# A two-layer graph kernel: the second pass in a written order, one more column chunk by lists, and the own-row logits in layer two

## The chip, the cores and the metric

The kernel runs on one core of one Trainium2 chip. Its time is the device time of one execution in microseconds (us), the median of several runs. Before the change it is 734.61 us, the median of three runs.

## The reference, cut to what matters

The graph has 3327 nodes, padded to 3328 = 26 blocks of 128; `adj` is sparse with denser first rows and columns. A node has 512 features.

```
h  = relu(layernorm(x))
x1 = x + adj @ (relu(adj @ (h @ W1) + b1) @ W2) + b2       # layer one, 128 hidden features
h1 = relu(layernorm(x1))
attn_a = sigmoid([adj @ h1, h1] @ Wa + ba);  attn_b likewise with Wb, bb
e  = where(adj != 0, exp(-leaky_relu(s_left[i] + s_right[j])), 0)   # s = (h1 @ W_sa) @ a_sa
x_a = e / (rowsum(e) + 1e-5) @ (h1 @ W_sa);  x_b = adj @ (h1 @ W_gcnb) + b_gcnb
out = x1 + sigmoid(attn_a * x_a + attn_b * x_b)
```

## The kernel before

The transposed matrix `adjT` lies in DRAM. Everything is float32, except the small tables from which lists are made. Columns are taken in chunks of 512, with one chunk of 256; `back` is their order, from the right to the left. Tile pools and dependencies are set by a scheduler: `queued(x)` puts what is written under it behind instruction x in its engine's order, `high_priority` ahead of others, and `pace(g, m)` makes a DMA wait for a matmul.

*First pass.* Rows of x are normalised and multiplied by W1 while chunk 0 is worked on. Then for each chunk the 26 blocks of `adjT` are loaded (`load_adj`, SyncE's queue, 256 KB each) and multiplied (`acc_u`, L568) into g = relu(adj @ u + b1), which `make_g` keeps and also stores to DRAM. VectorE takes for each block the largest value in every 32 columns (`most`, L572). From `most` of a finished chunk `make_lists` builds, during the next chunk, lists of the rows that have something in a group of 32 columns: VectorE flags and counts (L443 to L459), TensorE and VectorE turn the counts into row numbers (`at` L502, `p_list` L513, `past` to `row_a`, L519 to L532). GpSimd then gathers those pieces of `adjT` by indirect DMA (`ae`, L166). `rooms[i]` is the number of lists of 64 rows that a block has; a block in `OWN` (`extra` 1) takes its own diagonal block whole instead. If a list overflows, a fallback at the end computes everything again.

*Second pass.* `listed_chunks` are the first `LISTED` = 2 chunks of `back`: for them adj @ g is summed from the gathered pieces and gathered rows of g (`list_sums`, `acc_s`, L784). The others, `dense_chunks`, are loaded again and multiplied (`acc_g`, L825): five chunks, 130 products. For each finished chunk a generator `make_h1` makes its rows of layer two: load x and add b2 (L650), multiply by W2 (`px`, L663), add (L666), normalise (`ln_relu`: bn_stats, Sqrt, Relu), take two scores with `w_rows` (L623), store x1 and the row h (`store_row`), own logits with `w_own` (L630) for the blocks outside `OWN` and `LATE`, and turn the scores (`pl`, L687). Between the dense products the loop calls `next_late`, `next(summing)`, `next(hubs)` and `make_e_hub` by fixed counts. `add_hubs` sums block 0 of layer two (the hub, dense in every row) from `a_hub` and `e_hub` (`acc_hub`, L709). ScalarE goes back and forth between Sqrt for rows and Exp for `e_hub`.

*Layer two.* The other blocks go from 25 down to 1. For block i `attend` gathers the rows of h by list (`hr` or `rows`, 266 KB each pair half), makes e with `s_left` and stores it beside the adjacency in `ae`; `sums` multiplies (`acc`, L981); `turn` transposes (`ptt`, L995) and VectorE copies (`tyT`, L1010); `weigh` multiplies by `W_g_sb` (`p_b`, L1035) and `W_sa_sb` (`p_a`, L1042); `finish` makes the output. TensorE's order is: weigh one block, turn the next, sum a third. `fetch_ae` gathers two more pieces of `ae` a block.

Of the kernel before, what the change touches and what calls it, by code (L numbers as in the profile page):

```python
# [9 lines left out]
F32 = mybir.dt.float32  # L10
# [15 lines left out]
EH = 8  # L26
SEG = 4
WAKE = 14
LISTED = 2
LN_EPS = 1e-5  # L30
SUM_EPS = 1e-5
# [7 lines left out]
LATE = 10, 11, 16  # L39

OWN = 1, 6, 7, 8, 12, 13, 14, 15, 17, 18


def list_rooms(n_blocks):

    rooms = [0, 8, 7, 6, 5, 5] + 6 * [4]
    return (rooms + n_blocks * [3])[:n_blocks]
# [3 lines left out]
def kernel(  # L51
# [24 lines left out]
    if NP % CW:  # L76
        back.append((0, NP % CW))
    listed_chunks = back[:LISTED]
    ND = listed_chunks[-1][0]
    dense_chunks = [(c0, min(CW, ND - c0)) for c0 in range(0, ND, CW)]  # L80
    made_order = []
    for k, c in enumerate(dense_chunks):
        for c0, w in (c, *listed_chunks[k : k + 1]):
            made_order += range(c0 // P, (c0 + w) // P)
# [3 lines left out]
    extra = [int(i in OWN) for i in range(NB)]  # L88
# [29 lines left out]
    bab_row = kept([P, 2], "bab_row")  # L118
    w_own = kept([P, 2, D], "w_own")
# [20 lines left out]
    def segments(i):  # L140

        r = rooms[i] + extra[i]
        n = -(-r // SEG)
        cuts = [-(-r * k // n) for k in range(n + 1)]
        return list(zip(cuts, cuts[1:]))
# [50 lines left out]
    def load_own(i):  # L196

        n = segments(i)[0][1]
        for h in range(2):
            rows = slice(i * P + h * HALF, i * P + (h + 1) * HALF)  # L200
            nc.scalar.dma_start(
                ae[i][h * HALF : (h + 1) * HALF, 0 : n + 1 : n, :GW],
                adjT[rows, rows].rearrange("j (q i) -> j q i", i=GW),
            )
# [41 lines left out]

    def masked_exp(e, adj):
# [11 lines left out]
    with (  # L259
        tc.tile_pool(name="l0", bufs=1) as l0,  # L260
        tc.tile_pool(name="l0w", bufs=2) as l0w,
        tc.tile_pool(name="adjp", bufs=8) as adjp,
    ):

        def load_adj(j, c, name, n=1):

            c0, w = c
            t = adjp.tile([P, CW], F32, tag="adj", name=f"{name}_{c0}_{j}")
# [19 lines left out]
        def load_hub(k):  # L288
            rows = slice(k * NB // HUB_LOADS * P, (k + 1) * NB // HUB_LOADS * P)
            nc.scalar.dma_start(  # L290
# [4 lines left out]
        def load_weights():  # L295
            nc.scalar.dma_start(W2_sb, W2)
            nc.scalar.dma_start(b2_row, b2.partition_broadcast(P))
            nc.scalar.dma_start(W_sa_sb, W_sa.rearrange("(k p) f -> p k f", p=P))
            nc.scalar.dma_start(w_own, w_self.partition_broadcast(P))
            nc.scalar.dma_start(bab_row, b_ab.partition_broadcast(P))  # L300
# [6 lines left out]
        def load_x(i):  # L307
            xs[i] = l0w.tile([P, D], F32, tag="x", name=f"x_{i}", bufs=5)
            x_loaded[i] = nc.sync.dma_start(xs[i], x[i * P : (i + 1) * P, :])
# [46 lines left out]
        def kept0(shape, name, dtype):  # L356
            return l0.tile(shape, dtype, tag=name, name=name)
# [16 lines left out]
        def make_constants():  # L374
# [36 lines left out]
            for r in sorted(set(rooms[1:])):  # L411
                i0, n = rooms.index(r), rooms.count(r)
# [9 lines left out]
                )  # L422
            yield
# [9 lines left out]
        def make_lists(nth, most):  # L433
# [5 lines left out]
            def small(shape, name, dtype, bufs=2):  # L439
                return l0w.tile(shape, dtype, tag=name, name=f"{name}_{c0}", bufs=bufs)  # L440

            flag = small([P, MG, NB], "flag", BF16)
            nc.vector.tensor_scalar(flag[:, :n, :], most[:, :n, :], 0.0, None, op0=ALU.is_gt)  # L443
            for b in range(w // P):
                if extra[c0 // P + b]:
                    groups = slice(b * NQ, (b + 1) * NQ)
                    own = flag[:, groups, c0 // P + b]
                    nc.vector.tensor_tensor(own, own, apart, ALU.mult)

            upto = small([P, MG, NB], "upto", BF16)  # L450
            flat = "p b j -> p (b j)"
            nc.vector.tensor_tensor_scan(
                upto[:, :n, :].rearrange(flat), begin[:, :n, :].rearrange(flat),
                flag[:, :n, :].rearrange(flat), 0.0, op0=ALU.mult, op1=ALU.add,
            )
            count = small([P, MG], "count", BF16)
            nc.vector.tensor_copy(count[:, :n], upto[:, :n, NB - 1])
            after = small([P, MG, NB], "after", BF16)
            nc.vector.tensor_tensor(  # L459
                after[:, :n, :], count[:, :n].unsqueeze(2).to_broadcast([P, n, NB]),  # L460
                upto[:, :n, :], ALU.subtract,
            )
# [5 lines left out]
            nc.vector.tensor_copy(offset[:, :n], p_off[:, :n])  # L468
# [10 lines left out]
            nc.vector.tensor_tensor(  # L479
                step[:, :n, :NB], p_sh[:, : n * NB].rearrange("p (b j) -> p b j", j=NB),  # L480
                upto[:, :n, :], ALU.add,
            )
# [7 lines left out]
            for batch in batches:  # L490
# [6 lines left out]
                at = l0w.tile([P, CW // NT, 2, HALF], BF16, tag="at", name=f"at_{f0}")  # L497
# [20 lines left out]
                past = l0w.tile([P, CW // NT, NB], BF16, tag="past", name=f"past_{f0}", bufs=1)  # L518
# [4 lines left out]
                jb = l0w.tile([P, CW // NT], F32, tag="jb", name=f"jb_{f0}")  # L523
# [25 lines left out]
        for n, c in enumerate(back):  # L549
            c0, w = c  # L550
            acc = bank(psA, f"acc_u_{c0}")
            per = CW // w
            most = l0w.tile([P, MG, NB], F32, tag="most", name=f"most_{c0}")
            for j in range(NB):
# [9 lines left out]
                if j % per == 0:  # L564
                    with queued(x_loaded[min(j + 4, NB - 1)] if n == 0 else None):
                        tile_a = load_adj(j, c, "a1", per)
# [755 lines left out]
```

## Time and profile before

| what | us |
|---|---|
| median of three runs (731.07 to 735.44) | 734.61 |
| profiled execution | 834.5 |
| its span | 832.8 |
| first pass, chunk 0 (0 to 62) | 62 |
| first pass, the rest (62 to 237) | 175 |
| second pass and hub's end (237 to 490) | 253 |
| layer two (490 to 833) | 343 |
| TensorE busy | 735.6 |
| VectorE busy | 506.0 |
| GpSimd busy | 461.1 |

The profile is one execution, and it took 100 us more than the median of the runs. In the names of its lines L568 is line 568 of the kernel before. A float32 product on TensorE shows as two records. The recorded length of a matmul is modelled, so the distance between starts says more than the length.

### The profile page before, as it was taken

What the parts mean: (1) busy time and instruction counts of PE and PEld (TensorE: products, weight loads), DVE (VectorE), ACT (ScalarE), POOL (GpSimd) and SP (SyncE); (2) the same over time, 40 slices, a digit from 0 to 9 for tenths busy, and PEclk for the clock granted to TensorE, in tenths of its full rate; (3) what the DMA queues carried; (4) which work ended last, traced back from release to release, by engine and by line L of the source; (5) the groups of instructions that cost most, each with busy time, mean ns of one, the idle gap of its engine ahead of it and who ended that gap; (6) DMA issues with size and microseconds to landing.
All of it is one profiled execution on the core that took longest, in us unless ns stands there. A gap on an engine that the chain in (4) does not pass through costs nothing.

```text
span 832.8 us, 11907 instructions
## 1 busy us (share of the span) xinstructions
PE 735.6 (88%) x3595; PEld 404.5 (49%) x3595; DVE 506.0 (61%) x1625; ACT 194.5 (23%) x402; POOL 461.1 (55%) x490
## 2 busy tenths in 40 slices
PE   9999888989899771999899749967999999999995
PEld 7774333444543220444355236633656655665554
DVE  7778868898860611798987225523665557553552
ACT  7770000000000110354544002211212222221121
POOL 2201756766657776534456766674657666767500
PEclk9999989999999875999999969996999999999999
DMA  8788988988878844789994755664667877767510
GB/s 271 245 287 259 326 246 242 293 272 246 232 232 284 262 132 134 240 279 312 327 314 135 241 150 145 199 185 115 195 211 244 255 206 233 240 205 234 178 51 29
DMA packets 104889, 185.08 MB, mean 222 GB/s; under 512 B 18401, under 2 KB 35441, under 8 KB 104818
## 3 DMA queue, kind: packets, MB, share of 16 engines
q1 hardware_dynamic: 66544, 113.43, 41.8%
q0 software_dynamic: 23264, 57.64, 24.3%
q10 hardware_dynamic: 15010, 13.18, 4.9%
q8 instruction: 30, 0.49, 0.2%
q14 instruction: 41, 0.34, 0.1%
HBM read 162.29 MB, written 22.26 MB: 222 GB/s over the span
## 4 chain that ended last, share of the span: by engine, by line
PE 72%; DVE 7%; issue 6%; another core or an unknown queue 6%; DMA 5%; ACT 2%; POOL 1%; SPq 1%; DVEq 0%; ACTq 0%; POOLq 0%
PE acc_u L568 17%; PE acc L981 12%; PE p_b L1035 11%; PE p_a L1042 10%; PE acc_g L825 8%; PE pu L333 3%; PE ptt L995 3%; DMA a<-in_adjT_dram 2%; PE acc_hub L709 2%; PE px L663 2%; PE pt L325 1%; DMA xb<-in_x_dram 1%; PE acc_s L784 1%; DMA hr<-h_rows,row_h 1%
## 5 line engine op out<-in xcount | busy, mean ns | idle before, releaser
L166 POOL DMA_INDIRECT ae<-in_adjT_dram,row_a x194 | 202.6, 1044 | 181.8 <-DVE past L519 54.3
L568 PE MATMUL acc_u<-a,rows 128*128 128x512 f32 (+1 forms) x364 | 161.0, 583 | 0.5 <-DMA a<-in_adjT_dram 0.5
L166 POOL DMA_INDIRECT hr<-h_rows,row_h x120 | 122.7, 1022 | 62.5 <-issue 27.4
L825 PE MATMUL acc_g<-a,g 128*128 128x512 f32 (+1 forms) x260 | 117.1, 584 | 7.2 <-DMA a<-in_adjT_dram 6.8
L572 DVE TENSOR_REDUCE most<-a 128x16 f32<-128x512 f32 (+1 forms) x182 | 112.3, 638 | 11.6 <-issue 6.3
L1035 PE MATMUL p_b<-W_g_sb,tyT 128*128 128x257 f32 x416 | 99.3, 391 | 15.8 <-DVE tyT L1010 15.3
L1035 PEld LDWEIGHTS p_b<-W_g_sb,tyT 128*128 128x128 f32 x416 | 77.8, 192 | 46.5 <-DVE tyT L1010 15.6
L166 POOL DMA_INDIRECT rows<-h_rows,row_h x74 | 75.1, 1015 | 44.3 <-PE acc L981 20.9
L568 PEld LDWEIGHTS acc_u<-a,rows 128*128 128x128 f32 x364 | 67.2, 195 | 58.8 <-issue 56.0
L1042 PE MATMUL p_a<-W_sa_sb,tyT 128*128 128x512 f32 (+2 forms) x216 | 94.2, 577 | 0.2
L1010 DVE COPY tyT<-ptt 128x512 f32<-128x512 f32 x51 | 34.8, 685 | 87.0 <-PE p_a L1042 31.7
L825 PEld LDWEIGHTS acc_g<-a,g 128*128 128x128 f32 x260 | 50.0, 200 | 58.5 <-issue 44.9
L981 PE MATMUL acc<-hr,ae 64*64 64x512 f32 x480 | 68.3, 614 | 4.4 <-issue 4.0
L166 POOL DMA_INDIRECT g_row<-g_rows,row_h x48 | 49.0, 1021 | 20.9 <-issue 13.4
L1042 PEld LDWEIGHTS p_a<-W_sa_sb,tyT 128*128 128x128 f32 x216 | 40.7, 189 | 38.8 <-issue 36.9
L884 ACT ACTIVATE f<-f 128x2 f32<-128x2 f32 x26 | 5.3, 203 | 192.4 <-DVE f L883 97.2
L981 PEld LDWEIGHTS acc<-hr,ae 64*64 64x64 f32 x480 | 27.6, 136 | 33.6 <-issue 33.0
L343 ACT ACTIVATE gT<-acc_u,b_col 128x512 f32<-128x512 f32 (+1 forms) x7 | 4.6, 656 | 163.8 <-DMA a<-in_adjT_dram 90.9
L663 PE MATMUL px<-W_sb,sT 128*128 128x512 f32 x52 | 26.7, 650 | 15.4 <-ACT sT L799 12.0
L666 DVE TENSOR_TENSOR xb<-px,xb 128x512 f32<-128x512 f32 x26 | 17.3, 682 | 36.6 <-PE px L663 28.5
L981 PE MATMUL acc<-rows,ae 64*64 64x512 f32 x296 | 37.1, 593 | 2.5 <-issue 2.3
L623 DVE SCALAR_TENSOR_TENSOR junk<-rows,w_rows 128x512 bf16<-128x512 f32 x52 | 35.6, 684 | 3.2 <-ACT rows L244 1.1
(159 smaller groups left out, 945.2 us busy)
## 6 DMA issues: line engine op xcount, KB each, us to landing
a<-in_adjT_dram SPq DMA_DIRECT2D x286, 256.0 KB
h_rows<-rows SPq DMA_DIRECT2D x26, 260.0 KB
x<-in_x_dram SPq DMA_DIRECT2D x26, 256.0 KB
xb<-in_x_dram SPq DMA_DIRECT2D x26, 256.0 KB
x<-xb ACTq DMA_DIRECT2D x26, 256.0 KB
x1b<-x SPq DMA_DIRECT2D x26, 256.0 KB
out_dram<-va SPq DMA_DIRECT2D x25, 256.0 KB
ae<-in_adjT_dram,row_a POOLq DMA_INDIRECT x194
```

Of the source, the lines that this page charges most:

```text
L166: return nc.gpsimd.indirect_dma_start(out=dst, out_offset=None, in_=table, in_offset=bass.IndirectOffsetOnAxis(ap=rows, axis=0), bounds_ch ...
L333: nc.tensor.matmul(pu[:, :HID], hT[:, k, :], W1_sb[:, k, :], start=(k == 0), stop=(k == KD - 1))
L568: added = nc.tensor.matmul(acc[:, :w], u[j], a[:, :w], start=(j == 0), stop=(j == NB - 1))
L572: nc.vector.tensor_reduce(most[:, : w // GW, j], a[:, :w].rearrange("p (b i) -> p b i", i=GW), axis=AX.X, op=ALU.max, apply_absolute_value ...
L623: return nc.vector.scalar_tensor_tensor(junk, h, 1.0, w_rows[:, s, :], op0=ALU.mult, op1=ALU.mult, accum_out=into)
L663: last_row[2] = nc.tensor.matmul(px, sT[:, b * P : (b + 1) * P], W2_sb, start=True, stop=True)
L825: added = nc.tensor.matmul(acc[:, :w], g[j], a[:, n % per, :], start=(n == 0), stop=(n == NB - 1))
L981: added = nc.tensor.matmul(taken[i]["acc"][h][q * HALF : (q + 1) * HALF, :], both[half_p, q * n + k, :], taken[i][k0][k][half_p, q, :D], s ...
L995: moved = nc.tensor.transpose(pt[:, k * P : (k + 1) * P], ty[h][:, k * P : (k + 1) * P], ident)
L1010: last = nc.vector.tensor_copy(dst, src)
L1035: nc.tensor.matmul(p_b[n][:, :WH], tyT[:, k, 0, :], W_g_sb[:, k, n * WH : (n + 1) * WH], start=(k == 0), stop=(k == KD - 1),)
L1042: last = nc.tensor.matmul(p_a[:, c0:c1], tyT[:, k, 1, :], W_sa_sb[:, k, c0:c1], start=(k == 0), stop=(k == KD - 1),)
```

## The change

- `LISTED` goes from 2 to 3: columns 1792 to 2303 are summed from lists. Four dense chunks and three listed ones are left, 104 dense products. Blocks 9, 21 and 24 (`TOP`) take besides their own block also the upper half of block 0 whole (`g_top`, `h_top`, `extra` 2), and their rooms shrink to 3, 2 and 2. The last 256-column part and its neighbour change places: the chunks at 256 and 768 are swapped in `back`.
- First pass: `load_adj` takes 512 KB; `most` is taken for two blocks in one instruction; the flags and counts of `make_lists` get high priority on VectorE, and lists start from row 4 (`LISTS_FROM`) of the next chunk instead of row 2. The loads of W2, W_sa (in four), the hub's column (in five) and the own blocks are issued one by one behind matmuls over the pass (`load_behind`), not together at a chunk's end.
- Second pass: the order of dense products `d`, list sums `s`, `t`, rows `x`, turned scores `l`, hub products `h` and `e_hub` `e` is written out in `PLAN`, and TensorE keeps it. A gather is issued for each 1.4 us of planned TensorE time. x is loaded ahead into eight buffers. A row's sum comes with the addition, its squares from ScalarE, and Ln and Exp replace Sqrt, in one table set. Only five blocks take their left score here, and none its own logits.
- Layer two: hub products, the turn and p_b of block 0 are interleaved before the sums of blocks 25 and 24, and p_a of block 0 follows those. Each block loads its own row (`load_row`); `own_scores` takes its left score and own logits on VectorE one block ahead, and `turn_score` turns the score on TensorE.

The diff, cut to its core:

```diff
-LISTED = 2
+LISTED = 3
+LISTS_FROM = 4
+MADE = "dldldld"
+PLAN = """
+d26 s1 d2 x1 d1 x1 d3 s1 x1 l1 d3 x1 e2 s1 d8 s1 d3 t1 d3 x1 s1 x1 e2 d7 x1 s1 d3 x1 e2 d4 s1
...
+SPACE, QUIET = 1.4, 8.0
-LATE = 10, 11, 16
-OWN = 1, 6, 7, 8, 12, 13, 14, 15, 17, 18
+TOP = 9, 21, 24
+OWN = TOP + (1, 6, 7, 8, 12, 13, 14, 15, 17, 18)
...
+    rooms = [0, 8, 7, 6, 5, 5, 4, 4, 4, 3, 4, 4] + n_blocks * [3]
+    rooms[21] = rooms[24] = 2
...
+    back[-3:-1] = back[-2], back[-3]
...
+    def ln_relu_by_sum(dst, src, ln):
+        nc.vector.tensor_scalar(ln[:, 1:2], ln[:, 0:1], -1.0 / D, None, op0=ALU.mult)
+        nc.scalar.activation(dst, src, AF.Square, bias=ln[:, 1:2], accum_out=ln[:, 2:3])
+        nc.scalar.activation(ln[:, 3:4], ln[:, 2:3], AF.Ln, bias=eps, scale=1.0 / D)
+        nc.scalar.activation(ln[:, 4:5], ln[:, 3:4], AF.Exp, scale=-0.5)
+        nc.vector.tensor_tensor(ln[:, 0:1], ln[:, 1:2], ln[:, 4:5], ALU.mult)
+        return nc.scalar.activation(dst, src, AF.Relu, bias=ln[:, 0:1], scale=ln[:, 4:5])
...
-        tc.tile_pool(name="adjp", bufs=8) as adjp,
+        tc.tile_pool(name="adjp", bufs=6) as adjp,
...
+        def load_behind(added, n, j):
+            def load(out, in_):
+                pace(nc.scalar.dma_start(out, in_), added)
+            if j == 3 and n <= HUB_LOADS:
+                load_hub(n - 1, load)
+            if j == 13:
+                load_weights(n - 1, load)
+            if n > 1 and j in (6, 10, 16, 19, 22):
+                for i in own_order:
+                    load_own(i, load)
+                    break
...
+            with tc.high_priority():
+                flag = small([P, MG, NB], "flag", BF16)
...
+                both = 2 if n else 1
+                if j % both == 0:
+                    tiles = tile_a[:, j % per : j % per + both, :]
...
-                if j >= 2:
+                if j >= LISTS_FROM * CW // w:
                     next(lists, None)
...
+        def make_row():
+            i = next(made)
+            load_next()
+            add_b2()
+            x1 = xs.pop(i)
+            assert place[i] - NR < len(e_added)
+            with tc.high_priority():
+                px = bank(psB, f"px_{i}")
+                with behind_pe():
+                    on_pe[0] = last_row[2] = nc.tensor.matmul(
+                        px, sTs.pop(i), W2_sb, start=True, stop=True
+                    )
+                ln = l0w.tile([P, 5], F32, tag="ln5", name=f"ln_b{i}", bufs=3)
+                nc.vector.scalar_tensor_tensor(
+                    x1, px, 1.0, x1, op0=ALU.mult, op1=ALU.add, accum_out=ln[:, 0:1]
+                )
...
+        for what in plan:
+            does[what]()
+            owed[0] += STEP[what]
+            left -= STEP[what]
+            if owed[0] >= SPACE and left > QUIET:
+                owed[0] -= SPACE
+                gather_one()
...
+        def own_scores(i):
+            if i not in s_left:
+                nc.vector.scalar_tensor_tensor(
+                    junk, h_own[i][:, :D], 1.0, w_left, op0=ALU.mult, op1=ALU.mult,
+                    accum_out=node[i][:, 0:1],
+                )
+            own_logits(i, h_own[i], junk)
...
-        for i in range(NB - 2, 1, -1):
+        for i in range(NB - 3, 1, -1):
             with queued(*held):
+                load_row(i - 1)
                 for seg in segments(i):
                     made = attend(i, seg)
-            if i == NB - 2:
-                own_of(LATE[2], made[0])
+                own_scores(i - 1)
...
+            with queued(added):
+                added = turn_score(i - 1) or added
```

## The prediction

> **What bounds the kernel now.** I read the page first (sections 1, 2, 4), then the stage table, TensorE's timeline, and the waits, SyncE's queue included.
>
> ```profile
> span 832.8 us, 11907 instructions
> PE 735.6 (88%) x3595; PEld 404.5 (49%) x3595; DVE 506.0 (61%) x1625; ACT 194.5 (23%) x402; POOL 461.1 (55%) x490
> ...
> PE 72%; DVE 7%; issue 6%; another core or an unknown queue 6%; DMA 5%; ACT 2%; POOL 1%; SPq 1%; DVEq 0%; ACTq 0%; POOLq 0%
> ```
>
> TensorE is 88% busy and 72% of the chain that ended last. So matmuls removed count nearly in full, and other work counts where it holds TensorE up.
>
> ```profile
> 62.00:237.00 175.00, 156.53 (x740) 75.94 (x740) 148.02 (x390) 4.86 (x8) 103.64 (x101) 0.95 0.86 261
> 237.00:490.00 253.00, 198.79 (x711) 91.41 (x710) 138.69 (x460) 69.99 (x127) 150.51 (x144) 0.89 0.73 238
> 490.00:833.00 343.00, 319.97 (x1766) 189.93 (x1766) 173.07 (x619) 73.26 (x163) 195.28 (x192) 0.96 0.60 182
> ```
>
> The stage table has length, then busy time of TensorE, its weight loads, VectorE, ScalarE and GpSimd, clock, DMA share, GB/s. The rows are the first pass after its first chunk, the second pass with the hub block's end, and layer two. The first pass keeps VectorE 148 of 175 us busy, almost as long as TensorE. The second pass is slack: 253 us for 199 of TensorE.
>
> The profiled execution took 834.5 us, the median of the runs is 734.61. Where are the 100 us? I add TensorE's least time from spacings of starts: to the end of chunk 0, 63; first pass 145 (five chunks of 26 products at 0.87 us, one of 26 at 0.43, some 20 for lists and turns); second pass 181 (104 products at 0.87, 26 at 0.43, 26 px and 52 hub products at 0.86, 8 for list sums, 5 turns); layer two 317 (26 blocks of 3.67 p_b, 3.43 p_a, 1.09 turn, and 428 sums at 0.233, 5 for row sums); 8 of tail, 2 outside the span. Sum 716. So the timed runs hold only about 19 us of waiting, and most of the pauses of the profile (12 us at 321, 15 at 475, 12 around 560) belong to that execution. I take from it durations and short waits whose releaser is named, leave out the long pauses, and apply the sum of differences to the median.
>
> ```profile
> 168.54 0.30 PE L513 MATMUL p_list<-step,at 128*64 128x27 bf16 x7
> 169.35 0.27 PE L513 MATMUL p_list<-step,at 128*64 128x27 bf16 x5 [0.51 <-DVE at L502]
> 170.41 0.48 PE L513 MATMUL p_list<-step,at 128*64 128x27 bf16 x6 [0.79 <-DVE most L572]
> 171.44 0.49 PE L513 MATMUL p_list<-step,at 128*64 128x27 bf16 x6 [0.55 <-issue]
> ...
> 218.35 0.91 PE L513 MATMUL p_list<-step,at 128*64 128x27 bf16 x15 [2.08 <-DVE at L502]
> ...
> 355.72 0.32 PE L687 MATMUL pl<-ident,node 128*128 128x128 f32 x1 [2.22 <-DVE junk L623]
> ...
> 403.78 1.12 PE L663 MATMUL px<-W_sb,sT 128*128 128x512 f32 x2 [2.46 <-DVE xb L666]
> ```
>
> These are the short waits: list products held by VectorE, the turn of scores held by a row's score, px held by a late row. Brackets give the idle time and its releaser.
>
> ```profile
> 642.26 0.69 DVE L1010 COPY tyT<-ptt 128x512 f32<-128x512 f32 x1 [2.97 <-PE p_a L1042]
> 653.93 0.69 DVE L1010 COPY tyT<-ptt 128x512 f32<-128x512 f32 x1 [3.44 <-PE p_a L1042]
> ...
> SPq L935 <- PE acc L981: 45.4, 6, 9.1
> SPq L900 <- DVE va L899: 263.8, 21, 45.5
> ```
>
> In layer two the block period is 653.93 - 642.26 = 11.67 us, TensorE runs without gaps, and VectorE idles about 3.4 us before each tyT copy. SyncE's queue waits on outputs and on free buffers.
>
> **What the Trainium skill says.** (1) *Perfetto Trace Analysis*, Tensor Engine Instruction: TensorE's end is estimated from the instruction's size. The trace agrees: L568 records are 0.614 us, but 26 span 11.36, 0.437 apart; so I use spacings. (2) *VectorE: DVE Perf Modes*, "The TRN2 errata": each instruction pays a fixed cost. The reduce L572 takes 676 ns for 512 columns and 408 for 256: 268 ns for 256 columns, 140 fixed. (3) *ScalarE: Activation LUTs*, "What ACT_TABLE_LOAD costs": 1283 ns, and a drain; the table loads of L238 and L250 take 1283. (4) *DMA: Bandwidth & Descriptors*, "Latency and other measured facts": about 1 us first byte on GpSimd's path. Gathers here take 1.00 and start 1.30 apart.
>
> **The change part by part.**
> - *Third listed chunk.* Dense products of 512 columns fall from 104 to 78: 26 x 0.87 = -22.6 us. Small products acc_s rise from 100 to 168 (block groups of 12 take 0.79 us, 0.066 each): +4.5. Four more turns pt_s: +0.4. Top rows taken whole instead of listed lift the layer-two sums from 428 to 440: 12 x 0.233 = +2.8. 12 fewer list products: -0.3. Sum **-15.2 us**, all on TensorE.
> - *List flags first, pairs of rows in one reduce, lists from row 4, two chunks swapped.* List products lose 2.8 us (168.5 to 171.9, 24 records instead of 0.5), 2.5 at 197, 2.2 at 216 and 0.8 at 225: 8.3. Pairing saves 13 x 0.14 = 1.8 us of VectorE a chunk, and two more products (1.7 us) stand ahead of the lists. The swap puts the lists of blocks 2 to 5 beside a chunk of 512 columns, not of 256. I take two thirds: **-5.5** (bounds 0 and -8.3).
> - *Loads of W_sa, hub parts and own blocks spread out, 512 KB loads.* Same bytes. They wait for a product on ScalarE's queue; behind them there stands only the chunk's gT, and ScalarE is busy 5 of 175 us. 0; bounds -4 and +3, by the one 4.72 us DMA wait on the chain at 89.6.
> - *x six rows ahead, written order, row sums by ScalarE, one table set.* The waits of px and pl (2.2, 2.5, 0.8: 5.5) mostly go: **-4**. VectorE loses, a row, bn_stats 0.68, aggregate 0.16, one score 0.76, and for 13 rows 1.7 of own logits: some 64 us of 139. ScalarE gains a Square (about 0.8, as L244) and two small ones a row, 36 us, and loses 17 of its 24 table loads, 22 us; it has 70 of 253 busy. If the written order is wrong somewhere TensorE stands in it: **+3** for a few such places (0 to +10).
> - *Hub end.* Before, TensorE idles 2.4 us ahead of acc (471.1) and some 1.7 for two tyT copies. After, hub products and p_b of block 0 fill both: **-3** of 4.1. The second-pass work covers the 1 MB W_g_sb load: 22 products x 0.86 = 19 us lie between the last rows and p_b. Without that cover at 238 GB/s its 4.4 us show.
> - *Own logits, scores and 16 more own-row loads in layer two.* VectorE gains 2 x 0.76 + 0.15 for 16 blocks and 0.76 for 21: 43 us over 24 blocks, 1.8 a block, at most 2.45, against 3.4 idle. Hidden, less the crowded first blocks: **+2**. ScalarE's 42 small copies are hidden (73 of 343 busy); turns only change places. New wait: the row score waits for its 260 KB load; behind it on VectorE stand the tyT copies that TensorE needs next. SyncE issues that load behind x1b loads and output stores.
> - *Gathers.* 444 instead of 436: 8 x 1.30 = 10 us of GpSimd. In the second pass 113 paced by TensorE's planned time; 113 x 1.30 = 147 us inside some 165. In layer two 230 x 1.30 = 299 inside 320. Hidden; 0, up to +18 below.
>
> Sum: -15.2 - 5.5 - 4 + 3 - 3 + 2 = -22.7. Against the profiled 834.5 that is 812, if its pauses stayed; on the median 734.6 - 22.7 = **712**.
>
> **Rivals.**
> A. *More comes off.* VectorE, not TensorE, sets the first pass (148 against 157, and TensorE's busy time is modelled long): all 8.3, another 4 of DMA, all 4.1 of the hub's end and none of the +3 and +2: 712 - 2.8 - 4 - 1.1 - 5 = 699. For it: VectorE's load; against: no two engines in step ever lose every wait.
> B. *Gathers take the place of the dense products.* Twelve list sums each wait for rows; at 1.5 us a step (one gather's start-to-start and a little) +18: 730, no measurable change. For: 68 g rows instead of 48, and GpSimd is then about 90% taken in the second pass. Against: 24 buffers and a pace of 1.4 us, over 1.30.
> C. *Layer two turns to waiting for own rows: slower.* Place: VectorE's row score ahead of the tyT copies. Each of 21 blocks waits 2 us for a load that SyncE let stand behind an output: +42, 754. It decides from 1.1 us a block, where the gain is gone, and is slower by over 1% from 1.4. For: the 45.4 and 263.8 us of SyncE's waits; against: ten own blocks load in this way already, and the blocks around 642 run at full pace.
> D. *A listed block has more rows than its shortened room*, so that the whole fallback runs and the time is multiplied. The inputs' counts fit the new rooms; under 1%.
>
> **How the numbers follow.** Forecast 0.62, A 0.14, B 0.13, C 0.11. A measurement of this kernel can tell about 1% from no change: 727.3 to 742.0. The likeliest case spans 704 to 722 by the bounds above; A lowers the end to 697, B and the mild part of C raise it to 735. Faster: the forecast, A and a little of B, 0.78; same: most of B and the mild part of C, 0.12; slower: the rest, 0.10.
>
> **What would show it.** Right: 78 wide acc_g products; no p_list wait over 1 us; no table load between rows; p_b of block 0 directly behind hub products; a period of some 11.7 us in layer two with VectorE still idle over 1 us before tyT. Wrong: idle time before acc_s by gathers (B), before tyT or pl by h_own (C), a second pass whose TensorE work is not 15 us shorter, or first-pass chunks as long as before.

## The result, and the profile after

The changed kernel takes 734.55 us (median of 20 runs, 731.61 to 739.78), the kernel before 735.43 us (20 runs, 729.78 to 741.7): a ratio of 1.0002, 95% interval 0.9979 to 1.0025. No change can be measured; 712 was forecast. The profiled execution of before that the prediction read (834.5 us) is like those of one chip on which the kernel before itself takes 836 us; here the kernel before is read from a second profile of it (run e0_before_again, 735.04 us), and its stages can then be set beside those of after.

The page after: the span, the busy times, and the shares of the chain that ended last.

```profile
span 736.3 us, 11882 instructions
PE 694.0 (94%) x3695; PEld 383.0 (52%) x3695; DVE 482.2 (65%) x1505; ACT 201.0 (27%) x490; POOL 478.5 (65%) x516
PE 70%; DMA 16%; DVE 7%; ACT 3%; issue 1%; POOL 1%; SPq 1%; ACTq 0%; DVEq 0%; POOLq 0%
```

The same of the second profile of before:

```profile
span 733.3 us, 11907 instructions
PE 699.6 (95%) x3595; PEld 390.1 (53%) x3595; DVE 507.2 (69%) x1625; ACT 193.7 (26%) x402; POOL 467.2 (64%) x490
PE 67%; DMA 13%; DVE 7%; issue 5%; POOL 4%; ACT 2%; SPq 0%; POOLq 0%; ACTq 0%; DVEq 0%
```

TensorE was 95% busy already. It lost only 5.6 us of busy time, where the forecast took 15 us of products away, and idles 8.6 us more (736.3 - 694.0 against 733.3 - 699.6). Where it happens, the stage tables show: first pass from its second chunk on, second pass to the end of the last hub product in it, and the rest. Columns: stretch, length, busy time of TensorE, its weight loads, VectorE, ScalarE, GpSimd, TensorE's clock, DMA share, GB/s. First before, then after.

```profile
63.00:214.80 151.80, 143.74 (x720) 68.26 (x719) 141.87 (x375) 4.39 (x7) 100.15 (x99) 1.00 0.95 293
214.80:413.10 198.30, 187.70 (x696) 88.10 (x694) 139.56 (x463) 67.84 (x123) 141.28 (x132) 0.98 0.89 293
413.10:733.30 320.20, 307.45 (x1799) 186.40 (x1798) 179.09 (x629) 74.90 (x167) 214.03 (x207) 0.99 0.69 205
```

```profile
63.00:212.10 149.10, 143.10 (x706) 69.84 (x705) 138.50 (x311) 4.39 (x7) 97.94 (x95) 0.99 0.94 296
212.10:401.40 189.30, 170.16 (x767) 81.98 (x765) 92.28 (x320) 67.58 (x175) 134.18 (x130) 0.95 0.84 275
401.40:736.30 334.90, 319.62 (x1839) 183.40 (x1839) 204.07 (x716) 82.61 (x203) 233.54 (x221) 0.98 0.70 210
```

The first pass is 2.7 us shorter, the second 9.0, layer two 14.7 us longer. In the second pass TensorE has 17.5 us less to do (187.70 to 170.16), but half of it is handed back there: it stands idle, which is length less busy time, 19.1 us after against 10.6 before. TensorE's timeline after shows its long waits; brackets give the idle time ahead of an instruction and what ended it.

```profile
254.62 0.32 PE L749 MATMUL pl<-ident,node 128*128 128x128 f32 x1 [3.31 <-DVE junk L679]
...
303.07 0.48 PE L749 MATMUL pl<-ident,node 128*128 128x128 f32 x1 [5.11 <-DVE junk L679]
...
348.00 1.11 PE L894 MATMUL pt_s<-ident,s 128*128 128x128 f32 x4 [8.92 <-ACT s L889]
...
404.55 5.42 PE L1185 MATMUL p_b<-W_g_sb,tyT 128*128 128x257 f32 x16 [3.17 <-DVE tyT L1160]
```

VectorE's timeline ahead of the wait that ends at 303.07 shows what stands in front of the score (junk, L679):

```profile
294.96 0.29 DVE L276 SCALAR_TENSOR_TENSOR e_hub<-a_hub,e_hub 128x128 f32<-128x128 f32 x1 [0.50 <-ACT e_hub L275]
299.94 0.69 DVE L705 TENSOR_TENSOR xb<-xb,b_row 128x512 f32<-128x512 f32 x1 [4.68 <-DMA xb<-in_x_dram]
300.55 0.15 DVE L269 TENSOR_TENSOR ln_b<-ln_b 128x1 f32<-128x1 f32 x1
300.62 0.28 DVE L827 TENSOR_TENSOR es_hub<-es_hub,e_hub 128x128 f32<-128x128 f32 x1
301.58 0.69 DVE L679 SCALAR_TENSOR_TENSOR junk<-rows,w_rows 128x512 bf16<-128x512 f32 x1 [0.68 <-ACT rows L270]
```

The addition of b2 to a later x row (L705) waits 4.68 us for that row's load, and the normalization (L269), the Relu on ScalarE and the score of the row in work stand behind it. Over the second pass the waits read as follows (total, times, longest); the second line is SyncE's queue, where x loads wait for a buffer, that is for an x1 store.

```profile
DVE xb L705 <- DMA xb<-in_x_dram: 58.9, 24, 8.2
...
SPq L700 <- DMA x<-xb: 48.2, 13, 8.5
```

### The profile page after: what moved, and what is told of

Its sections match the earlier page's. It is cut to its first block, busy times and chain, and to the rows that moved or that the text cites. A ratio compares the mean times of both kernels' runs of the same rounds, so it can differ in the third digit from the quotient of the medians.

```text
span 736.3 us, 11882 instructions
## 1 busy us (share of the span) xinstructions
PE 694.0 (94%) x3695; PEld 383.0 (52%) x3695; DVE 482.2 (65%) x1505; ACT 201.0 (27%) x490; POOL 478.5 (65%) x516
## 4 chain that ended last, share of the span: by engine, by line
PE 70%; DMA 16%; DVE 7%; ACT 3%; issue 1%; POOL 1%; SPq 1%; ACTq 0%; DVEq 0%; POOLq 0%
PE acc_u L620 14%; PE acc L1131 14%; PE p_b L1185 13%; PE p_a L1193 12%; DMA xb<-in_x_dram 7%; DMA x<-xb 4%; PE acc_g L922 3%; PE pu L378 3%; PE ptt L1145 3%; DVE most L627 2%; PE acc_hub L772 2%; DMA a<-in_adjT_dram 2%; PE pt L370 2%; PE px L720 1%; DMA h_own<-h_rows 1%
## 5 line engine op out<-in xcount | busy, mean ns | idle before, releaser
L627 DVE TENSOR_REDUCE most<-a 128x32 f32<-128x1024 f32 (+1 forms) x104 | 103.2, 1007 | 10.6 <-DMA a<-in_adjT_dram 10.3
L180 POOL DMA_INDIRECT g_row<-g_rows,row_h x68 | 71.4, 1050 | 28.4 <-issue 12.5
L1160 DVE COPY tyT<-ptt 128x512 f32<-128x512 f32 x51 | 34.9, 685 | 79.4 <-PE ptt L1145 79.4
L922 PE MATMUL acc_g<-a,g 128*128 128x512 f32 (+1 forms) x208 | 85.5, 554 | 1.0 <-DMA a<-in_adjT_dram 1.0
L922 PEld LDWEIGHTS acc_g<-a,g 128*128 128x128 f32 x208 | 38.9, 193 | 39.4 <-issue 34.7
L705 DVE TENSOR_TENSOR xb<-xb,b_row 128x512 f32<-128x512 f32 x26 | 18.0, 692 | 58.9 <-DMA xb<-in_x_dram 58.9
L1131 PE MATMUL acc<-hr,ae 64*64 64x512 f32 x480 | 56.2, 593 | 0.0
L984 DVE SCALAR_TENSOR_TENSOR a_hub<-h_own,w_own 128x512 f32<-128x512 f32 x52 | 35.6, 684 | 10.6 <-DMA h_own<-h_rows 10.6
L1067 ACT COPY s_left<-pl 64x64 f32<-64x64 f32 x42 | 8.7, 207 | 118.7 <-PE pl L1063 118.5
L1131 PEld LDWEIGHTS acc<-hr,ae 64*64 64x64 f32 x480 | 19.5, 134 | 29.1 <-issue 25.5
L266 ACT ACTIVATE rows<-xb,ln_b 128x512 f32<-128x512 f32 x26 | 18.8, 722 | 48.6 <-DVE ln_b L265 43.0
```

What stands on the lines that cost most here:

```text
L180: return nc.gpsimd.indirect_dma_start(out=dst, out_offset=None, in_=table, in_offset=bass.IndirectOffsetOnAxis(ap=rows, axis=0), bounds_ch ...
L266: nc.scalar.activation(dst, src, AF.Square, bias=ln[:, 1:2], accum_out=ln[:, 2:3])
L627: nc.vector.tensor_reduce(most[:, : w // GW, j : j + both], tiles.rearrange("p k (b i) -> p b k i", i=GW), axis=AX.X, op=ALU.max, apply_ab ...
L922: on_pe[0] = nc.tensor.matmul(acc[:, :w], g[j], a[:, n % per, :], start=(n == 0), stop=(n == NB - 1))
L984: nc.vector.scalar_tensor_tensor(junk, h[:, :D], 1.0, w_own[:, s, :], op0=ALU.mult, op1=ALU.mult, accum_out=node[i][:, 1 + s : 2 + s],)
L1131: added = nc.tensor.matmul(taken[i]["acc"][h][q * HALF : (q + 1) * HALF, :], both[half_p, q * n + k, :], taken[i][k0][k][half_p, q, :D], s ...
```

## The experiments

Ratios are to runs of the kernel before on the same chip in the same series.

**e0_before_again**: the kernel before, unchanged.

> The kernel before, unchanged, for a second profiled execution: the first one took 834.5 us, 100 above the median of its runs, so its stages could not be read. Theory T1 (the third listed chunk and the list changes did shorten TensorE's work, and new waits in the second pass gave it back): first pass (62 us to the last product of the narrow chunk) about 155 us against 149 after; second pass about 181 to 185 us of TensorE work with under 8 us of idle, against 161 of work and some 22 of idle after; layer two 6 to 9 us shorter than after's. Theory T2 (the old kernel never waited, and the change saved less work than was reckoned): the second pass shows under 175 us in all, and the stages differ by less than 3 us each. Theory T3 (the pauses of the first profile are in every execution): the span is over 800 us again.

Measured: 735.04 us, span 733.3. T3 falls. Idle time of TensorE in the three stages, up to its last product: 8.1, 10.6 and 4.8 us before, 6.0, 19.1 and 6.3 after. T1 holds in kind, though idle time in the second pass was 10.6 us and not under 8, TensorE's busy time in it 187.7, not 181 to 185, and layer two 14.7 us shorter than after's, not 6 to 9.

**e1_b2_in_time**: the addition is put behind the px addition of the row before.

```
-            add_b2()
             x1 = xs.pop(i)
+            with queued(added_x[0]):
+                nc.vector.tensor_tensor(x1, x1, b2_row, ALU.add)
...
-                nc.vector.scalar_tensor_tensor(
+                added_x[0] = nc.vector.scalar_tensor_tensor(
```

> After, with the addition of b2 to an x row queued on VectorE behind the previous row's px addition, one row ahead instead of four to six. T1 (the addition, placed rows ahead in VectorE's in-order queue, waits for an x load whose buffer waits for an x1 store, and scores, s copy and pt_s stand behind it: 5.1 us at 299, 8.9 at 339 and parts of the waits near 256): the two long waits go, the second pass falls by 9 to 14 us, the time to about 722 to 727. T4 (the x loads are late because the 16 DMA engines are full between 214 and 305 us, share about 1.0): the row itself then waits for its load instead, TensorE waits the same at px, and the time stays within 3 us of 735. T5 (the order of the written list is too tight for the row's chain of about 4.4 us, whatever the loads do): pl keeps its waits of 3.3 and 5.1 us and the time falls by under 4 us.

Measured: 722.86 us, ratio 0.9854 (0.9813 to 0.9896), 11 us less than after (0.0148 x 733): T1. TensorE's waits in its second pass:

```profile
PE pt_s L895 <- ACT s L890: 1.4, 1, 1.4
PE acc_g L923 <- DMA a<-in_adjT_dram: 1.2, 2, 0.9
PE pl L750 <- DVE junk L679: 0.5, 1, 0.5
```

```profile
210.80:378.20 167.40, 164.21 (x767) 79.41 (x766) 91.70 (x325) 68.50 (x176) 129.92 (x124) 1.00 0.92 310
378.20:722.00 343.80, 320.85 (x1839) 182.57 (x1839) 202.62 (x712) 82.65 (x203) 238.33 (x227) 0.97 0.69 205
```

The second pass takes 167.4 us, 22 less than after, and the loads of the same bytes run at 310 GB/s: the DMA engines were no limit (T4 falls), nor was the written order (T5). But layer two grows by 9 us; its first sums now wait for VectorE's masked scores, which wait for gathered rows:

```profile
389.59 3.69 PE L1130 MATMUL acc<-rows,ae 64*64 64x512 f32 x16 [6.63 <-DVE ae L276]
```

**e2_x_bufs_12**: `X_BUFS = 12` in place of 8.

> After, with 12 buffers for x rows instead of 8 (nine loads ahead of the first row instead of five), the early additions left where they are. T1: the additions' loads no longer wait for x1 stores, so the waits at 299 and 339 go as in the run with the addition in time: 722 to 727. T4: four more loads of 256 KB fall into the stretch where the DMA engines are full, dense loads come later by 4 x 256 KB / 330 GB/s = 3.2 us, and the time stays or grows by up to 3 us. T5: under 4 us less.

Measured: 739.41 us, ratio 1.0105 (1.0066 to 1.0144); no theory had 5 us more from this alone. The additions wait as before (53.5 us, 21 times), and TensorE still waits 5.81 us for pl and 7.03 for pt_s. Its waits for dense loads grow from 1.0 us to 7.2, 4.58 of them at 240: so much of T4, that more x loads hold up dense ones, is seen. The order of VectorE's instructions tells why. Counting how many rows each addition stands ahead of the last px addition done (1 is directly ahead of its own row's px addition):

```
after, 8 buffers:  1 2 3 4 5 6 7 8 6 6 7 8 7 7 7 7 7 7 7 7 7 7 7 7 6 7
e2, 12 buffers:    1 2 3 4 5 6 7 8 9 10 11 11 10 10 11 11 11 11 11 ... 11
e1:                1 1 1 1 1 ... 1
```

So the additions were not left where they were: the scheduler places each as soon as its row has a buffer, and in most rows the lead is one less than the buffers. The "four to six" in the expectation of e1 was wrong too.

**e14_bufs_12_lead_7**: 12 buffers, and the lead held at seven.

```
-X_BUFS = 8
+X_BUFS = 12
...
-                nc.vector.tensor_tensor(xs[i], xs[i], b2_row, ALU.add)
+                with queued(added_x[place[i] - 7] if place[i] >= 7 else None):
+                    nc.vector.tensor_tensor(xs[i], xs[i], b2_row, ALU.add)
```

> The changed kernel with 12 buffers for x rows and the additions of b2 held where they were with 8, seven rows ahead (each queued on VectorE behind the px addition of seven rows earlier). T1 in its narrower form (an addition waits because its lead, one less than the buffers, needs the buffer that the x1 store has just freed): four rows lie now between the freed buffer and the addition, the waits at 299 and 339 go, and the time is that of the addition in time, about 723, ratio 0.985. T4 (x loads come late by themselves, DMA engines full): as with 12 buffers before, 735 to 739, ratio 1.00 to 1.01.

Measured: 724.83 us, ratio 0.9911 (0.9878 to 0.9944); its waits for pl and pt_s are under 0.6 us each, those for dense loads 6.1 us. Neither the early place as such nor a lack of buffers as such was the fault, but a lead that uses the buffers up. With 8 buffers the addition for row k+8 needs the store of row k's x1 (3.9 us to land in the median), which frees the buffer, and then a load into it (4.1): 8.0 us. In VectorE's order it stands only one row behind row k's px addition, and rows follow each other every 5.3 us (px additions from 248.4 to 382.1 for 26 rows). VectorE waits for about the difference: the 18 additions from the ninth row on, which need a freed buffer, wait 38.7 of the 58.9 us, 2.2 each; the rest is the wait for the first loads.

**e3_own_after_turn**: own logits of blocks 25 and 0 behind block 0's tyT copy.

```
-            for i in (NB - 1, 0):
-                own_scores(i)
             fetch_ae(AE_PER)
             with queued(added):
                 _, added, copied = turn(0, ty, False, tyT, (1,))
+            with queued(copied):
+                for i in (NB - 1, 0):
+                    own_scores(i)
```

> After, with the own logits of blocks 25 and 0 queued on VectorE behind the tyT copies of block 0 instead of ahead of them. They waited 10.55 us for their row load, and p_b of block 0 waited 3.2 us behind them (401.4 to 404.55). If that wait is what ends last there, the gap goes: 2.5 to 3.5 us less, about 732. If TensorE then waits for W_g_sb or for the hub sums instead, no change.

Measured: 734.53 us, ratio 1.003 (1.0 to 1.0061): nothing. p_b follows the hub products without a gap now, but the sums behind it wait 3.42 us for VectorE's masked scores instead. One wait took the place of another.

**First series on the chip where the kernel before takes 836 us**: e4, e5, e6 and e7, all built on e1.

```
e4:  -                if j % 4 if w == CW else j % 2:
     -                    gather_behind(added)
     +                gather_behind(added)
e5:  LISTS_FROM = 2; both = 1; no tc.high_priority() in make_lists
e6:  LISTED = 2; MADE = "dldlddd"; in PLAN 26 d in place of the third chunk's s and t
e7:  turn_score(i - 1) queued ahead of add_es() in the loop over blocks
```

> The kernel with the b2 addition in time (722.86 us), with a gather behind every product of the first pass that finds a list ready, instead of three of four. In that kernel GpSimd starts a gather every 1.30 us without a break from 354 us on, and TensorE waits 6.6 us at 389.6 and 2.3 + 0.8 us with slow products at 669 to 676 for rows. G1 (the gathers have become the bound: 444 x 1.30 = 577 us, and they can start only at about 125): more of them in the first pass, where GpSimd waits 63.7 us for the product that it follows, shorten the later waits: 4 to 9 us less, 714 to 719. G2 (lists, not the pace, hold the gathers of the first pass back): within 1.5 us of 722.9. G3 (the first pass has its DMA engines at 0.93, so the dense loads come later): 1 to 4 us more.

> The kernel with the b2 addition in time, with the list work of the first pass as before: no priority for the flags and counts on VectorE, one reduce a tile and not one for two, lists taken up from the third product on and not the fifth. The swap of chunks and the spread loads stay. The prediction put this part at 5.5 us (0 to 8.3): 728 us then. The two clean profiles speak for less: the first pass ends 2.6 us earlier after than before, with all its parts together: 1 to 3 us more, about 725. If the waits of the lists were never on the path: no change.

> The kernel with the b2 addition in time, with two chunks summed by lists in the second pass and not three: 26 more products of 512 columns there, 68 fewer small ones, four turns fewer, 20 g rows fewer to gather; the written order is kept, with the 26 products where the third chunk's list sums stood. The prediction's term for this, without the top rows and the lists: 22.6 - 4.5 - 0.4 = 17.7 us more. W (TensorE's work is what counts): 16 to 18 us more, about 740. G1 (gathers bound the kernel): 26 us less of GpSimd's work and 18 us more time to do it, so the waits for rows in layer two, some 9 us with their slow products, go, and it is only 7 to 10 us more, about 731.

> The kernel with the b2 addition in time, with the turn of the next block's score ahead of the one-column row sums on TensorE instead of behind them. In the kernel before, the row sums stood directly ahead of acc products on other rows of the array and took about 0.1 us a block with them; after, the turn stands between, and row sums and turn take 0.21 + 0.25 us a block. W: 21 blocks x 0.1 to 0.15 = 2 to 3 us less, about 720.5. G1: TensorE only waits longer for the rows then: no change. If the turn now waits for its score on VectorE (it comes 0.2 us earlier): slower by up to 4 us.

Measured there: 856.81 us (ratio 1.0272), 818.01 (0.9783), 799.86 (0.9579) and 822.73 (0.9771, from two of its four runs). In all four profiles TensorE's own instructions come late (waits put down to issue, as in the 834.5 us profile), so these ratios say nothing of the other chips. Three of the kernels were run again elsewhere; e7's edit only inside e8.

**e6b_two_listed**:

> The kernel with the b2 addition in time and two listed chunks once more: its first run fell on a chip on which the kernel before itself took 836 us, with pauses put down to issue in all its profiles, so that it tells nothing of a chip where it takes 733. W (TensorE's work is what counts): 16 to 18 us over 722.9, about 740, a ratio of 1.01 to the kernel before. G1 (gathers bound the kernel): about 731, a ratio of 0.996.

Measured: 735.9 us, ratio 1.0034 (1.0011 to 1.0057), against 0.9854 of e1: the third listed chunk is worth 0.018 x 733 = 13.2 us, some 3.5 us either way by the two intervals, where W had 16 to 18 and G1 7 to 10. TensorE is busy 14.3 us longer than in e1 (704.5 and 690.2) and idles 2.5 us less ahead of its last product.

**e5b_lists_as_before**:

> The kernel with the b2 addition in time and the list work as before once more, for the same reason. The prediction's step: 5.5 us more, ratio 0.993. The clean profiles: 1 to 3 us more, ratio 0.988. Never on the path: ratio 0.985.

Measured: 719.93 us, ratio 0.9786 (0.9736 to 0.9835), against 0.9854 (0.9813 to 0.9896). The list work as before costs nothing; it is rather 5 us better, with intervals that overlap. It has the longer wait for lists all the same: 2.92 us for p_list at 174, against 1.31 in e1.

**e9_lists_from_2**: e1 with `LISTS_FROM = 2` alone.

> The kernel with the b2 addition in time (ratio 0.985 to the kernel before), with lists taken up from the third product of a chunk as before, not the fifth; priority and paired reduce stay. G1 (GpSimd's stream of gathers is the bound): its first gather comes at 80 to 81 us and not 85.0, as in the run with all list work as before, and the time falls by 3 to 5 us, ratio 0.979. W (TensorE is the bound): within 1 us; two more products ahead of the lists hide their flags better, so that waits at p_off could even come back: ratio 0.985 to 0.987.

Measured: 721.19 us, ratio 0.9843 (0.9807 to 0.988). The first gather comes at 83.7 us, not 80 to 81, and the time is e1's. What made e5b's difference, if it is one, stays open.

**e4b_gathers_every_product**:

> The kernel with the b2 addition in time and a gather behind every product of the first pass once more. On the chip where the kernel before took 836 us it was slower by 2.7% than that kernel, where its sisters were 2.2% faster, so G3 (the first pass pays for it) has gained. G1: 714 to 719, ratio 0.976. G2: ratio 0.985. G3: 726 or more, ratio from 0.990.

Measured: 760.67 us, ratio 1.0346 (1.0294 to 1.0398), far beyond G3, and by another cause. TensorE's timeline:

```profile
266.00 0.64 PE L879 MATMUL acc_s<-g_row,ae 64*32 64x128 f32 x4 [26.14 <-DMA g_row<-g_rows,row_h]
```

In e1 already GpSimd starts a gather every 1.30 us from 85 us on, with no pause over 0.45 us. More adjacency gathers in its queue were not done sooner (94 start by 210 us in both runs); the rows of g that the list sums need stood behind them, and their first gather starts at 263.3 us, not 222.0.

**e8_three_edits**: e1, e3's and e7's edits together.

> Three edits together: the b2 addition in time, the own logits of blocks 25 and 0 behind the tyT copies of block 0, the turn of the next score ahead of the row sums. W (each takes its wait or its work from TensorE): 722.9 - 0.6 (the wait before p_b that is left with the addition in time) - 2.5 (turn) = 719 to 720.5, ratio 0.981. G1 (gathers bound layer two from its first sums to its last blocks): ratio 0.985, no gain over the addition in time alone.

Measured: 725.45 us, ratio 0.9869 (0.9816 to 0.9922): no gain over e1. The turn's edit does what W expected of it, and somewhat more: the block period falls from 12.03 to 11.78 us, and the acc products start beside the row sums again.

```profile
528.95 0.27 PE L1062 MATMUL pl<-ident,node 128*128 128x128 f32 x1
529.15 0.22 PE L1167 MATMUL p_b<-ones,es 64*64 64x1 f32 x2
529.17 0.65 PE L1130 MATMUL acc<-h_own,ae 64*64 64x512 f32 x2
```

TensorE is busy 4.8 us less than in e1 (685.4 and 690.2), but idles more: the opening waits 8.64 and 3.55 us, the last blocks 2.07 and 2.52.

**e10, e11, e12: 24 gathers left out**, in e1, after and before.

```
+                        if 2 <= i <= 13 and k == r + extra[i] - 1:
+                            continue
                         yield gather(
```

> The kernel with the b2 addition in time, with 24 of its 444 gathers left out: the last adjacency column group of blocks 2 to 13 isn't fetched and counts as zero; TensorE's and VectorE's instructions stay. G1: GpSimd has 24 x 1.30 = 31 us less, more than TensorE can use; the waits for rows at 389 and 669 shrink to those of the first gathers after the last h store: 5 to 10 us less, ratio 0.972 to 0.978. W: within 2 us, ratio 0.983 to 0.987.

> The changed kernel itself with the same 24 gathers left out (the last adjacency column group of blocks 2 to 13 counts as zero). In its profile TensorE waits for scores and s copies, not for gathers, and runs layer two at its own pace: T1 (the early b2 additions are what ends last): within 2 us of it, ratio 1.00. G1 in the strong form (gathers bound the changed kernel too): 5 to 10 us less, ratio 0.987 to 0.993.

> The kernel before with 24 of its 436 gathers left out (the last adjacency column group of blocks 2 to 13 counts as zero). Its last gather starts at 688.9 us, 44 us before the end, and TensorE runs its layer two at an even 11.67 us a block: if it is bound by TensorE, within 2 us, ratio 1.00. If gathers bound it as well: 4 us or more off, ratio under 0.995.

Measured: 720.77 us, ratio 0.9839 (0.9802 to 0.9875); 735.35, 1.0019 (0.9996 to 1.0042); 733.09, 1.0011 (0.9985 to 1.0037). With fewer gathers neither the kernel before nor the changed one gains, and e1 by 2 us, within its spread: e10's last blocks don't wait any more, but its opening still does, for 6.80 us. For the last blocks G1 falls as a bound. The opening this run does not test: up to 376 us e10 issues as many gathers as e1 (215 and 217), because others move up into the places that are left out. In e1 GpSimd is full all the same (444 gathers from 85.0 to 684.4 us), so it allows little more.

**e13_quiet_16**: e5b with `QUIET = 16.0` in place of 8.0.

> The kernel with the b2 addition in time and the list work as before (719.93 us, ratio 0.9786), with the paced gathers of the second pass ended 16 us of planned work before its end instead of 8. GpSimd then has no adjacency gathers queued when the last h row lands, and the six row gathers of block 25 can start some 6 us sooner. If the opening of layer two (waits of 5.9 and 2.3 us, slow products after them) is a place of its own: 4 to 7 us less, ratio 0.970 to 0.974. If GpSimd, without a break from 80 to 683 us, only shifts the wait to the last blocks: within 1.5 us, ratio 0.977 to 0.981.

Measured: 719.75 us, ratio 0.9836 (0.9795 to 0.9878). The wait at the opening falls from 5.94 to 3.13 us and waits of 1.99 and 0.83 us appear at 666 and 669: shifted, not saved. With e5b it has the lowest median, not to be told from e9 and e10; both beat both kernels.

## Why the prediction was wrong, step by step

TensorE's time from spacings of starts, before to after: work -5.3 us, idle +7.3. The rest of the +3.0 between the two profiled spans lies behind its last product. In that work is time lost to a slow clock, explained below: 3.4 us before, 11.2 after. At full clock the work fell by 5.3 + 7.8 = 13.1 us.

- **Third listed chunk, -15.2.** Right in mechanism, nearly right in size. The groups of TensorE that carry it (records are two to a product), before:

```profile
L825 PE MATMUL acc_g<-a,g 128*128 128x512 f32 x208 | 100.1, 616 | 2.2 <-DMA a<-in_adjT_dram 2.2
L784 PE MATMUL acc_s<-g_row,ae 64*32 64x128 f32 x192 | 7.5, 273 | 0.0
L687 PE MATMUL pl<-ident,node 128*128 128x128 f32 x26 | 5.1, 276 | 4.3 <-DVE junk L623 4.3
```

and after:

```profile
L922 PE MATMUL acc_g<-a,g 128*128 128x512 f32 x156 | 73.2, 611 | 1.0 <-DMA a<-in_adjT_dram 1.0
L879 PE MATMUL acc_s<-g_row,ae 64*32 64x128 f32 x272 | 9.7, 271 | 0.0
L1063 PE MATMUL pl<-ident,node 128*128 128x128 f32 x21 | 6.8, 323 | 0.0
```

  Dense products -24.0 by spacing (-22.6 forecast), list sums +4.0 (+4.5), turns pt_s +1.0 (+0.4), layer-two sums +3.9, some of it slow products (+2.8). e6b gives 13.2 us for the chunk alone.
- **List work, -5.5.** Wrong. The waits it was read from were those of the 834.5 us profile; in the clean one p_list, p_off and p_sh waited 4.0 us together. The first pass became 2.7 us shorter with all its parts, and e5b shows no gain from the list edits, the swap left aside, which was not tried by itself. One p_list wait of 1.28 us is left.
- **Spread loads, 0.** Not tried alone, but one wait came with them that the clean profile of before does not have:

```profile
118.84 0.66 PE L391 MATMUL pg<-ident,gT 128*128 128x128 f32 x4 [1.96 <-ACT gT L388]
```

  ScalarE's queue issues own-block loads until 118.05 us, and gT starts behind them at 118.10, 1.2 us after the chunk's last product. The prediction named gT as what stands behind these loads and priced it at nothing.
- **x six rows ahead and written order, -4 and +3 (0 to +10).** This step failed. "The waits of px and pl mostly go": px's did (none over 0.1 us after, 3.09 before), pl's went from 4.3 to 8.4 us and pt_s got 9.7. The loads were taken as "ahead"; nobody counted where the additions that depend on them stand in VectorE's order. With that mended the kernel gains: e1, 11 us, just outside the bound of +10 that was kept for a written order that is wrong somewhere. Then the -4 is there too: in e1 px, pl and pt_s wait 1.9 us together, before 8.4. VectorE was freed of 47 us in that stage (139.56 to 92.28) and ScalarE of 17 table loads (20 to 3; the prediction counted 24, and none is left between rows); what each of these gave was not separated.
- **Hub end, -3.** Wrong. 3.17 us of wait came where 4.1 were to go (2.56 and 0.35 in the clean profile): the own logits of block 25 stand ahead of block 0's tyT copy and wait 10.6 us for their row's load. That is rival C's mechanism, but once, at the opening, not in 21 blocks.
- **Own logits and turns in layer two, +2.** Mis-sized: "turns only change places" was wrong. Groups in layer two before, between a block's ptt and the next p_b:

```profile
527.54 1.04 PE L995 MATMUL ptt<-ident,ty 128*128 128x128 f32 x8
528.50 0.22 PE L1018 MATMUL p_b<-ones,es 64*64 64x1 f32 x2
528.52 0.65 PE L981 MATMUL acc<-h_own,ae 64*64 64x512 f32 x2
```

  and after:

```profile
512.31 1.04 PE L1145 MATMUL ptt<-ident,ty 128*128 128x128 f32 x8
513.28 0.28 PE L1168 MATMUL p_b<-ones,es 64*64 64x1 f32 x4
513.49 0.32 PE L1063 MATMUL pl<-ident,node 128*128 128x128 f32 x1
513.74 2.81 PE L1131 MATMUL acc<-hr,ae 64*64 64x512 f32 x24
```

  Before, the first acc product starts 0.02 us after the row sums, beside them; after, row sums (0.21) and a turn by itself (0.25) come one after the other. The block period rises from 11.67 to 12.03 us, and 21 x 0.36 = 7.5 us of layer two's 14.7 are this. The turns that left the second pass took 0.12 us each there (26 in 3.12), so the net is some 5 us more, not 2. e8 bears the reading out: with the turn ahead of the row sums the period is 11.78 us. VectorE stayed hidden, as forecast: it idles 79.4 / 24 = 3.3 us ahead of tyT.
- **Gathers, 0.** Right for this kernel, and with it rival B falls: its 730 us lies near the measured time by luck, for acc_s waits 0.0 us for its rows, and e11 gains nothing. e1 has little margin left: GpSimd is full there.

Of the prediction's signs of being right, the 78 wide acc_g products, the missing table loads and VectorE's idle time before tyT came; p_list waits 1.28 us, p_b of block 0 waits 3.17 behind the hub products, and the period is 12.03.

So of -22.7 us, 13 came, as work, and were used up: 7.3 us of idle time and 7.8 us of slow clock. The idle time was foreseen as a bound of +10; the clock was not in the sum at all. e1 and e14 show where 7 to 11 of the missing 22 us went. How far the list work, the hub's end and the turns fell short of their terms is read from profiles. The list edits (e5b), the own logits at the hub's end (e3) and, with two other edits, the turn (e8) were also tried, and undoing none of them shortened the kernel beyond the spread; how the rest of the 22 us divides stays open. *TensorE: Matmul & The Clock Gate* of the Trainium skill (Part 1, What's actually happening) says that TensorE falls to half clock after an idle window of about 3.4 us and comes back after a busy one. The trace agrees. After, around the wait of 8.92 us (the clock stands third from the end):

```profile
340.00:343.00 3.00, 0.00 (x0) 0.00 (x0) 0.75 (x2) 0.78 (x5) 2.21 (x3) 1.00 0.54 180
343.00:344.00 1.00, 0.00 (x0) 0.00 (x0) 1.00 (x5) 0.75 (x1) 0.81 (x1) 0.81 0.10 16
344.00:348.00 4.00, 0.00 (x0) 0.00 (x1) 2.61 (x12) 2.75 (x8) 0.00 (x0) 0.50 0.70 215
348.00:353.00 5.00, 5.00 (x9) 2.59 (x10) 3.26 (x11) 1.99 (x6) 1.20 (x2) 0.50 0.61 206
353.00:354.00 1.00, 1.00 (x3) 0.39 (x2) 0.60 (x5) 0.33 (x1) 0.80 (x1) 0.57 0.00 0
```

Products run at half clock for 5.9 us after it, 2.9 us lost. The p_b group at 404.55 took 5.42 us, not 3.74 as in e1, for the same reason. Summed as busy time times (1 - clock) over each microsecond: 3.4 us before, 11.2 after, 6.0 in e1.

## What to carry to other kernels

An instruction that waits for a load blocks its in-order engine: after a change in prefetch depth, count in the order of instructions how many rows ahead each consumer stands, and compare the lead with the buffers, for a scheduler may spend every buffer on placing it earlier. In a kernel that is 95% TensorE, price a wait of more than some two microseconds at its length and about half of 3.4 us after it, 1.7. And take pauses from a profile only when its span agrees with the timed runs; a second profile of the same kernel was worth more than the argument about the first.

## What the hardware showed unexpectedly

- Short waits can halve the clock as well: 2.15 us at 253 before was followed by 0.50 from 254 to 257, while 3.09 us at 348 before was not. The same section of the page has the window free-running, 3.413 us long, and the kept traces agree. Cut into windows of that length on one grid (before it passes 254.20 us, after 254.88), every window shows the clock at 1.00 or 0.50 and none between (211 and 3 before, 206 and 8 after). So a wait counts by how much of it falls into one window:

| profile | window from, us | idle in it, us | clock in the next |
|---|---|---|---|
| before | 250.79 | 2.15 | 0.50 |
| before | 295.16 | 2.76 | 0.50 |
| before | 342.95 and 346.36 (the wait of 3.09) | 1.14 and 1.95 | 1.00 |
| before | 411.21 and 414.63 (the wait of 2.56) | 1.51 and 1.06 | 1.00 |
| after | 108.11 | 1.82 | 1.00 |
| after | 411.89 (64-row sums) | 1.98 | 0.50 |
| after | 176.37 (31 small list products) | 1.59 | 0.50 |

  Idle time is not all that counts: after, the window at 725.92 has 2.01 us and full clock behind it. Windows filled with small products fall sooner here; what is measured in them stays open.
- GpSimd's gathers start 1.30 us apart over hundreds in a row, and they kept the order of their queue: surplus work given to it early made TensorE wait 26 us for what was needed first (e4b).
- The kernel before takes 733 us on three chips and 836 on another, with TensorE waiting for its own instructions there, and the ranking of variants changes with it (two listed chunks: ratio 0.958 there, 1.003 elsewhere).
